# Preparing the expert layer's token operands in units 4 to 7 and keeping them in DRAM, in a decoder layer on one Trainium2 core

## The chip, the cores and the metric

The kernel runs on one core of one Trainium2 (trn2) chip. The metric is the device time of one execution in microseconds (us). Six instruction streams matter here: PE (TensorE, the matmul engine, with its weight loads shown apart as PEld), DVE (VectorE), ACT (ScalarE), POOL (GpSimd), and SP, the queue from which nearly all DMA transfers are issued. Each engine works through its own instructions in order and waits at semaphores for the others.

## What is computed

A decoder layer over 2 x 2048 tokens of width 512, in float32: linear attention, cross attention on a short context, and a mixture of experts. Only the last part is touched by the change:

```python
def _L0_ffn_ref(hidden_states, router_w, w_gate, w_up, w_down, ws_gate, ws_up, ws_down):
    TOP_K = 6
    def _glu_mlp(x, wg, wu, wd):
        return jax.nn.silu(x @ wg) * (x @ wu) @ wd
    B, S, D, E, F, FS = (2, 1024, 512, 8, 256, 512)
    ...
    x = hidden_states.reshape(-1, D)
    scores = jax.nn.softmax(x @ router_w, axis=-1)
    topk_w, topk_idx = jax.lax.top_k(scores, TOP_K)
    g = jnp.einsum('td,edf->etf', x, w_gate)
    u = jnp.einsum('td,edf->etf', x, w_up)
    f_all = jnp.einsum('etf,efd->ted', jax.nn.silu(g) * u, w_down)
    ...
    y = jnp.sum(picked * topk_w[:, :, None], axis=1).reshape(B, S, D)
    y = y + _glu_mlp(hidden_states, ws_gate, ws_up, ws_down)
    return y
x = x + _L0_attn_ref(_layernorm(x, axis=-1), ...)
x = x + _L0_xattn_ref(_layernorm(x, axis=-1), ctx_1024, ctx_1024, ...)
x = x + _L0_ffn_ref(_layernorm(x, axis=-1), ...)
```

All eight experts are computed for every token; the router's softmax, cut to the six best experts, gives the weights (gates) of the sum. A shared expert is added.

## The kernel before

**Tiles and stages.** The 4096 tokens are eight blocks of `TB` = 512 tokens, each four tiles of 128 tokens. Attention and cross attention run first, block by block, and leave the residual stream of block b in DRAM as `x2[b]`. Then comes the expert stage, which starts at about 1042 us of the span. It takes the blocks in four groups of two (g = 0, 2, 4, 6). For each group it goes through ten units u: eight experts and the shared expert in two halves. That makes forty (group, unit) pairs n = 0 to 39, the list `todo3`; group 2 begins at n = 10, group 4 at n = 20, group 6 at n = 30.

**Exact matmuls in three terms.** An operand is held as a pair: a rounded high half (`nc.scalar.copy` into a float32r tile on ACT) and a low half, the original less the high half (`low`, line 118, on DVE or POOL). A product takes three matmuls (`TERMS`): high x high, low x high, high x low.

**Seven parts per unit.** The gate and up products of a unit for two blocks are made by a scheme of the Strassen-Winograd kind with `NP` = 7 products in place of 8. Part s (`products`, matmul at line 1053) multiplies a weight operand `wq` with a token operand `xo` of 128 x 1024 values in a pair (`xops[g, s]`). Two parts use the transposed tokens of the first block directly, one those of the second, four use sums and differences. Each part is 12 matmuls of 128x512, so a unit has 84. The down products add 42 per unit in the same form (`down_products`, line 1166, sums gathered on DVE at line 1187), interleaved with the next unit's parts. In group 0 (n = 0 to 9, "early") weights come raw and their operands are made on ACT, DVE and POOL and stored to DRAM for the later groups (`prepare`, `down_sums`), and down products take 48 matmuls per unit in plain form (`down`, line 148). Later groups load the finished weight operands (`load_until`, at most three uses ahead of program order).

**Preparing the next group, before the change.** In unit 8 of a group `expert_ahead(b)` loads the eight tiles of the next two blocks of `x2`, normalizes them (`normalize`, lines 245 to 252: statistics and scaling on DVE, a power on POOL; pinned in program order), turns them with PE transposes (line 802) and copies them with ACT into `raws[b]`, 8 KB per partition and block (line 803). Sixteen matmul ticks after a block's last tile `route(b)` makes its router scores (line 815), copies them out with DVE (`ls`, line 824), and 22 ticks later `rank(b, ls)` turns them back (line 833), takes the softmax and compares each expert with each other one to keep the best six (lines 842 to 861, DVE with two steps on POOL). `store_gates` writes the gates to DRAM (lines 871 to 875), from where later groups load them as rows (`gr`, line 1103). In unit 9 `tokens_part(g, s)`, called once after each part, makes the seven token operands for the next group out of `raws`: subtractions on POOL (line 1015), the high half on ACT (line 1035), the low half on DVE (line 118, tile `xo`).

**Order.** `dense` is a list of generators that emit PE's matmuls one by one; `dense.after(n, f)` calls f after n further matmuls. This sets the program order. The framework then orders each engine's instructions by a simulated timeline, with program order as priority; an instruction made under `keep_in_program_order` (also called `held`) stays in its place. DMA loads on SP can stand far ahead of their use, as far as free buffers allow.

**Buffers.** `big` has 17 buffers of 8 KB per partition (`eight`): token operands, weight operands, raw weights, `raws`. `work` has 4 pairs (`pair_of`, tag `hl`), 9 single tiles (`half`, tag `kp`) and 5 row tiles (tag `xs`, for loaded token tiles and gate rows). PSUM has 4 banks for parts (`ps`) and 4 for everything else (`sc`).

Of the kernel before, what the change touches and what calls it, by code (L numbers as in the profile page):

```python
# [17 lines left out]
P = 128  # L18
# [19 lines left out]
def decoder_layer(  # L38
# [62 lines left out]
    def half(name, dtype=F32):  # L101
        return work.tile([P, 512], dtype, tag="kp", name=name, bufs=9)
# [664 lines left out]
    for s in range(ws_gate.shape[1] // F):  # L767
# [14 lines left out]
        base=0,  # L782
        channel_multiplier=0,
    )
    accs, raws, gates = {}, {}, {}
# [24 lines left out]

    def route(b):

        pl = sc.tile([P, TB], F32, tag="sc", name=f"pl{b}")
        for k in range(NC):
            nc.tensor.matmul(
                pl[k * HD : (k + 1) * HD, :],
                lhsT=rw[:, k, :],
                rhs=raws[b][:, k, :],
                start=True,
                stop=True,  # L820
                skip_group_check=True,
            )
        ls = half(f"ls{b}")
        nc.vector.tensor_copy(ls, pl)
        dense.after(22, lambda: rank(b, ls))

    def rank(b, ls):


        gates[b] = small.tile([P, NT, E], F32, tag="gates", bufs=4, name=f"gates{b}")  # L830
        pr = sc.tile([P, NT, NC, HD], F32, tag="sc", name=f"pr{b}")
        for t in range(NT):
            nc.tensor.transpose(
                pr[:, t].rearrange("p k e -> p (k e)"), ls[:, t * P : (t + 1) * P], ident
            )
        wide = [P, NT, E]

        def little(tag, shape):
            return small.tile(shape, F32, tag=tag, name=f"{tag}{b}", bufs=1)

        lg = little("lg", wide)
        nc.vector.tensor_reduce(lg, pr[:, :, :, :E].rearrange("p t k e -> p t e k"), AX.X, ALU.add)
        m = little("m", [P, NT])
        nc.vector.tensor_reduce(m, lg, AX.X, ALU.max)
        s = little("s", wide)
        nc.vector.tensor_tensor(s, lg, m.unsqueeze(2).to_broadcast(wide), ALU.subtract)
        nc.scalar.activation(s, s, AF.Exp)
        nc.vector.tensor_reduce(m, s, AX.X, ALU.add)
        nc.vector.reciprocal(m, m)
        nc.vector.tensor_tensor(s, s, m.unsqueeze(2).to_broadcast(wide), ALU.mult)  # L850
        rk = little("rank", wide)
        mine = s.unsqueeze(3).to_broadcast([P, NT, E, E])
        other = s.unsqueeze(2).to_broadcast([P, NT, E, E])
# [4 lines left out]
        nc.gpsimd.tensor_tensor(eq, eq, before.unsqueeze(1).to_broadcast([P, NT, E, E]), ALU.mult)  # L858
        nc.gpsimd.tensor_tensor(gt, gt, eq, ALU.add)
        nc.vector.tensor_reduce(rk, gt, AX.X, ALU.add)  # L860
        nc.vector.scalar_tensor_tensor(gates[b], rk, float(TOPK), s, ALU.is_lt, ALU.mult)
        if b >= GROUP:
            dense.after(60, lambda: store_gates(b))

    gated = {g: dram.tile([E, GROUP, TB], F32, name=f"gated{g}") for g in range(GROUP, nblk, GROUP)}

# [17 lines left out]
    todo3 = [  # L884
        (range(g, g + 2), u) for g in range(0, nblk, 2) for u in range(len(units))
    ]
    NP = 7
    KH = NC // 2
    quarter = [P, 2, KH, P]
    DH = D // 2  # L890
    LAST = len(todo3) - 1
# [116 lines left out]

    def tokens_part(g, s):

        lo, hi = slice(0, KH), slice(KH, NC)

        def less(dst, a, b):
            if g:
                held(nc.gpsimd.tensor_tensor(dst, a, b, ALU.subtract))
            else:
                nc.vector.tensor_tensor(dst, a, b, ALU.subtract)

        r0, r1 = raws[g], raws.get(g + 1)
        xop = xops[g, s] = eight([P, 2, KH, TB], FR, f"xo{g}_{s}")  # L1020
# [436 lines left out]
    for n, (group, u) in enumerate(todo3):  # L1457
        early_group = n < len(units)
        g = group[0]
        more = group[-1] + 1 < nblk  # L1460
        ahead = [[], []]
        if u == len(units) - 2 and more:
            ahead = [expert_ahead(b) for b in range(group[-1] + 1, group[-1] + 3)]
        parts = products(n) if n else ready
        downs = [[] for _ in range(NP)]
        if n > len(units):
            downs = [[d] for d in down_products(n - 1)]
        if u == 1 and n > len(units) + 1:
# [119 lines left out]
```

## Time and profile before

| what | value |
|---|---|
| median of three runs | 2346.76 us (2346.34 to 2348.77) |
| the profiled execution | 2340.21 us |
| its span in the trace | 2338.5 us |
| mean granted PE clock | 0.984 |
| DMA traffic | 485.63 MB, mean 208 GB/s |
| chain that ended last: PE at line 1053 (`pg`) | 25% of the span |
| the same, PE at line 1166 (`pf`) | 10% of the span |
| first part of unit n = 0, 10, 20, 30 starts at | 1042.3, 1417.5, 1715.8, 2021.8 us |

The page counts an engine as busy while one of its instructions runs; matmuls are pipelined, so a busy PE can still run slowly. A wait is put down to the instruction whose semaphore came last. The expert stage takes 1296 of the 2338.5 us. A window is a stretch of the span; its row gives each engine's busy time in it.

### The profile page before, as it was taken

How to read it: one execution, taken by the hardware profiler on the slowest of the kernel's cores; microseconds unless marked ns; L12 is line 12 of the kernel's file. 1: busy time of each engine (PE TensorE's matmuls, PEld its weight loads, DVE VectorE, ACT ScalarE, POOL GpSimd, SP SyncE). 2: the span in 40 equal slices, each digit the busy share in tenths (PEclk: the TensorE clock that was granted, in tenths of full speed). 3: DMA queues.
4: the chain of work that ended last, by engine and by line, in shares of the span. 5: the costliest groups of instructions: out<-in, count | busy, mean ns of one | idle time of the engine just before them, and what ended most of it. 6: DMA issues, size and time to landing. Idle time of an engine off the chain costs nothing.

```text
span 2338.5 us, 35133 instructions
## 1 busy us (share of the span) xinstructions
PE 2241.0 (96%) x11978; PEld 1733.3 (74%) x11978; DVE 1680.3 (72%) x2777; ACT 1104.9 (47%) x2598; POOL 1223.2 (52%) x1086
## 2 busy tenths in 40 slices
PE   7999999899989999999999999999999999999999
PEld 5888777655577777766777777888778887788887
DVE  6554555668577776877877786777887778977777
ACT  4555776756566766775343333222333222432221
POOL 5545433547475554553655554544564455754543
PEclk9999999999999999999999999999999999999999
DMA  6555778899965665565665646555447556575553
GB/s 210 180 171 174 208 210 228 248 255 266 258 201 159 173 175 155 172 199 203 243 240 221 223 175 258 209 222 207 158 180 275 207 207 236 193 276 202 211 189 131
DMA packets 194896, 485.63 MB, mean 208 GB/s; under 512 B 26970, under 2 KB 46810, under 8 KB 174782
## 3 DMA queue, kind: packets, MB, share of 16 engines
q1 hardware_dynamic: 192990, 477.30, 61.5%
q0 software_dynamic: 1728, 6.09, 0.9%
q8 instruction: 95, 1.56, 0.3%
q14 instruction: 83, 0.68, 0.1%
HBM read 345.01 MB, written 138.31 MB: 207 GB/s over the span
## 4 chain that ended last, share of the span: by engine, by line
PE 48%; DVE 9%; DMA 5%; POOL 4%; issue 3%; ACT 2%; SPq 0%; ACTq 0%; DVEq 0%; POOLq 0%
PE pg L1053 25%; PE pf L1166 10%; PE po_x L148 3%; PE pf L148 2%; PE xpq L148 2%; PE pc L745 2%; PE xpt L725 1%; PE psc L693 1%; DMA rgu<-in_w_up 1%; DVE u L1073 1%; DVE xo L118 1%; POOL hp L118 1%; DVE wq L118 1%; DVE u L1085 1%; DMA xsx<-x 1%
## 5 line engine op out<-in xcount | busy, mean ns | idle before, releaser
L1053 PE MATMUL pg<-xo,wq 128*128 128x512 f32 x3360 | 825.7, 393 | 7.2 <-ACT s L1064 3.5
L1053 PEld LDWEIGHTS pg<-xo,wq 128*128 128x128 f32 x3360 | 630.2, 189 | 149.3 <-ACT s L1064 7.1
L1187 DVE TENSOR_TENSOR sum<-sum,pf 128x512 f32<-128x512 f32 x376 | 250.5, 682 | 61.1 <-PE pf L1166 53.5
L407 POOL TENSOR_TENSOR kacc<-kacc,e_k 128x512 f32<-128x512 f32 x128 | 165.9, 1297 | 225.6 <-DVE e_k L366 203.6
L703 ACT ACTIVATE xe<-psc,nb 128x154 f32<-128x154 f32 x512 | 194.4, 403 | 63.0 <-DVE nb L700 47.4
L708 POOL TENSOR_TENSOR xe<-xe,sm 128x616 f32<-128x616 f32 x128 | 156.7, 1232 | 108.1 <-DVE sm L707 73.7
L1116 POOL TENSOR_TENSOR u<-u,gr 128x512 f32<-128x512 f32 x48 | 63.8, 1328 | 255.7 <-DVE u L1085 244.3
L1166 PE MATMUL pf<-ht,wdo 128*128 128x512 f32 x696 | 187.4, 393 | 1.0 <-DVE sum L1187 1.0
L366 DVE SCALAR_TENSOR_TENSOR e_k<-pp,e_k 128x512 f32<-128x512 f32 x128 | 87.4, 685 | 107.9 <-ACT e_k L365 101.8
L1166 PE MATMUL pf<-hb,wdo 128*128 128x512 f32 x522 | 148.2, 399 | 6.0 <-DVE sum L1187 5.9
L1166 PEld LDWEIGHTS pf<-ht,wdo 128*128 128x128 f32 x696 | 129.8, 188 | 30.7 <-DVE sum L1187 1.7
L1084 ACT ACTIVATE u<-u 128x512 f32<-128x512 f32 x80 | 50.6, 633 | 211.1 <-DVE u L1073 208.5
L148 PE MATMUL pf<-wd,hp 128*128 128x512 f32 x528 | 134.0, 400 | 6.2 <-DVE hp L118 3.0
L700 DVE TENSOR_REDUCE nb<-psc 128x2 f32<-128x308 f32 x256 | 111.9, 467 | 31.1 <-PE psc L693 30.9
L148 PEld LDWEIGHTS pf<-wd,hp 128*128 128x128 f32 x528 | 99.7, 190 | 33.1 <-DVE hp L118 3.9
L1166 PEld LDWEIGHTS pf<-hb,wdo 128*128 128x128 f32 x522 | 97.4, 189 | 30.4 <-DVE sum L1187 7.7
L1073 DVE TENSOR_TENSOR u<-u,pg 128x512 f32<-128x512 f32 x160 | 107.7, 679 | 10.5 <-PE pg L1053 9.7
L703 ACT ACTIVATION_READ_ACCUMULATOR xe<-psc,nb 128x1 f32 x512 | 111.6, 218 | 0.0
L364 ACT ACTIVATE e_k<-pp 128x512 f32<-128x512 f32 x128 | 76.8, 601 | 69.9 <-PE pp L402 64.4
L693 PEld LDWEIGHTS psc<-xkst,xst 96*128 96x128 f32 x512 | 76.1, 193 | 35.2 <-ACT xe L703 18.9
L693 PE MATMUL psc<-xkst,xst 96*128 96x154 f32 x512 | 90.3, 284 | 12.3 <-ACT xe L703 8.4
L402 PEld LDWEIGHTS pp<-pst,kst 96*128 96x128 f32 x512 | 75.8, 191 | 26.8 <-issue 9.9
(280 smaller groups left out, 5143.2 us busy)
## 6 DMA issues: line engine op xcount, KB each, us to landing
wq<-wqs SPq DMA_DIRECT2D x90, 1024.0 KB
wqs<-wq SPq DMA_DIRECT2D x30, 1024.0 KB
wdo<-wds SPq DMA_DIRECT2D x29, 1024.0 KB
kst<-kd SPq DMA_DIRECT2D x96, 256.0 KB
qst<-qd SPq DMA_DIRECT2D x96, 256.0 KB
xst<-xqd SPq DMA_DIRECT2D x96, 256.0 KB
wdo<-wds SPq DMA_DIRECT2D x29, 768.0 KB
kd<-khl SPq DMA_DIRECT2D x32, 512.0 KB
```

Of the source, the lines that this page charges most:

```text
L148: nc.tensor.matmul(dst, lhsT=a, rhs=b, start=n == 0, stop=n == len(todo) - 1)
L364: nc.scalar.activation(e, src, AF.Relu, scale=-1.0)
L366: nc.vector.scalar_tensor_tensor(e, src, 0.0, e, ALU.max, ALU.add)
L407: nc.gpsimd.tensor_tensor(acc, acc, kp, ALU.add)
L693: nc.tensor.matmul(psc[:, i], lhsT=xsts[b, c][:, h, t * P : (t + 1) * P], rhs=ksts[bt, c][:, h, :], start=True, stop=True,)
L700: nc.vector.tensor_reduce(nb[:, two], psc, AX.X, ALU.max, negate=True)
L703: nc.scalar.activation(e[:, h, :], psc[:, i], AF.Exp, bias=nb[:, h : h + 1], accum_out=sm[:, h : h + 1],)
L708: nc.gpsimd.tensor_tensor(e, e, sm.unsqueeze(2).to_broadcast([P, 4, keys]), ALU.mult)
L1053: nc.tensor.matmul(pb, lhsT=w[:, p, i, k, :], rhs=xop[:, q, k, :], start=first and m == 0, stop=m == len(todo) - 1, skip_group_check=True,)
L1073: nc.vector.tensor_tensor(dst, dst, pb, ALU.add)
L1166: nc.tensor.matmul(banks[i], lhsT=w[:, p, i * P : (i + 1) * P], rhs=t[q], start=new and m == 0, stop=m == len(TERMS) - 1, skip_group_check ...
L1187: nc.vector.tensor_tensor(dst, dst, banks[i], ALU.add)
```

## The change

The preparation of groups 2, 4 and 6 is taken apart into small pieces and spread over earlier units:

- **Layernorms** of blocks 2 to 7 (`normalize_ahead`): one tile at a time, 24 in all, at parts 2 and 5 of units n = 0 to 3 and at part 5 of units n = 4 to 19. The normalized tile is stored in DRAM (`xn2`). They are no longer pinned.
- **Token operands** of the next group (`operands_ahead`): 24 pieces, one after each part from part 1 of unit 4 to part 3 of unit 7. They come in two halves q of 12 pieces: four that load and turn tiles of `xn2` (a quarter of the next two blocks' values each, as 16 loads of 128 KB per group), one for router scores, seven for the operands. A half operand is 128 x 512, made by ACT and DVE in a `pair_of` tile and stored in DRAM (`xod`); eight subtractions of 128 x 512 per group run on POOL.
- **Unit 9**: `tokens_part` for later groups only loads the finished operand, one DMA of 1 MB.
- **Routing**: the scores of two blocks stand in one tile of double width; softmax and ranking run once per group instead of once per block, with single steps further apart. This holds for group 0 too, where one `routed(0)` takes the place of two. Scores are copied out by ACT instead of DVE.

The diff, without the parts that only move:

```diff
+    xod = {}
+    xn2 = {b: dram.tile([TB, D], F32, name=f"xn2_{b}") for b in range(GROUP, nblk)}
...
-            xs = load_tile(x2[b], 0, t, f"f{b}_")
-            made[t] = normalize(xs, f"f{b}_{t}", pinned=b > 1)
+            made[t] = normalize(load_tile(x2[b], 0, t, f"f{b}_"), f"f{b}_{t}")
...
-            if t == NT - 1 and b > 1:
-                dense.after(16, lambda: route(b))
...
+    def normalize_ahead(b, t):
+        xs = normalize(load_tile(x2[b], 0, t, f"n{b}_"), f"n{b}_{t}")
+        dense.after(8, lambda: nc.sync.dma_start(out=tile_of(xn2[b], 0, t), in_=xs))
+        yield from ()
+
+    def operands_ahead(g):
+        turned, tiles, firsts = {}, {}, []
+
+        def load(q, j, t2):
+            xs = work.tile([P, 2, 2, P], F32, tag="xs", name=f"xq{g}_{q}_{j}_{t2}", bufs=5)
+            for i in range(2):
+                nc.sync.dma_start(
+                    out=xs[:, i],
+                    in_=tile_of(xn2[g + j], 0, 2 * t2 + i).rearrange(
+                        "p (h q n) -> p h q n", h=2, q=KH
+                    )[:, :, q],
+                )
+            tiles[q, j, t2] = xs
+
+        def turn(q, j, t2):
+            if (j, t2) == (0, 0):
+                turned[q] = eight([P, GROUP, 2, TB], F32, f"xt{g}_{q}")
+            xs = tiles.pop((q, j, t2))
+            pt = sc.tile([P, 2, 2, P], F32, tag="sc", name=f"ptf{g}_{q}_{j}_{t2}")
+            for h in range(2):
+                for i in range(2):
+                    nc.tensor.transpose(pt[:, h, i, :], xs[:, i, h, :], ident)
+            nc.scalar.copy(
+                turned[q][:, j, :, 2 * t2 * P : 2 * (t2 + 1) * P],
+                pt.rearrange("p h i n -> p h (i n)"),
+            )
...
+        def scores(q):
+            pl = sc.tile([P, TB], F32, tag="sc", name=f"pl{g}_{q}")
...
+            ls = half(f"ls{g}_{q}")
+            nc.scalar.copy(ls, pl)
+            dense.after(14, lambda: add_scores(q, ls))
+            yield from ()
...
+        def operand(q, n):
+            (b11, b21), (b12, b22) = ([turned[q][:, j, h] for h in range(2)] for j in range(GROUP))
+
+            def less(dst, a, b):
+                nc.gpsimd.tensor_tensor(dst, a, b, ALU.subtract)
+
+            if n == 2:
+                less(b11, b12, b11)
+                src = half(f"t2_{g}_{q}")
+                less(src, b22, b11)
+                less(b21, b21, src)
+            elif n == 3:
+                less(b12, b22, b12)
+                src = b12
+            else:
+                src = (b11, b21, None, None, b21, b11, b22)[n]
+            hl = pair_of(f"xo{g}_{n}_{q}")
+            nc.scalar.copy(hl[:, 0], src)
+            low(hl[:, 1], src, hl[:, 0])
+            dense.after(
+                6, lambda: nc.sync.dma_start(out=xod[g, n][:, :, q, :], in_=hl.bitcast(F32))
+            )
+            yield from ()
+
+        parts = []
+        for q in range(KH):
+            parts += [turns(q, n) for n in range(4)] + [scores(q)]
+            parts += [operand(q, n) for n in range(NP)]
+        return parts
...
-        nc.vector.tensor_copy(ls, pl)
-        dense.after(22, lambda: rank(b, ls))
+            ls.append(half(f"ls{b + j}"))
+            nc.scalar.copy(ls[j], pl)
+        dense.after(14, lambda: turn_scores(b, ls))
...
+        nc.scalar.activation(s, s, AF.Exp)
+        dense.after(14, lambda: rank(b, s, m))
...
-        both = half(f"gteq{b}").rearrange("p (i t e j) -> p i t e j", i=2, t=NT, e=E)
+        both = pair_of(f"gteq{b}").bitcast(F32)
...
+        dense.after(40 if b else 14, chosen)
...
+        xop = xops[g, s] = eight([P, 2, KH, TB], FR, f"xo{g}_{s}")
+        if g:
+            nc.sync.dma_start(out=xop.bitcast(F32), in_=xod[g, s])
+            return
...
-    dense.add(outs[0], routed(0), routed(1), outs[1], prepare(0, 1), tokens_part(0, 2), outs[2])
+    dense.add(outs[0], routed(0), outs[1], prepare(0, 1), tokens_part(0, 2), outs[2])
...
-        ahead = [[], []]
-        if u == len(units) - 2 and more:
-            ahead = [expert_ahead(b) for b in range(group[-1] + 1, group[-1] + 3)]
+        if u == 0 and more:
+            ahead = operands_ahead(group[-1] + 1)
...
-            if ahead[0]:
-                (ln, tr), (ln2, tr2) = ahead
-                todo = (ln, [], tr[:2], tr[2:] + ln2, [], tr2[:2], tr2[2:])
-                dense.add(*todo[s])
+            if s == 5 or s == 2 and n < 4:
+                at = 2 * n + s // 3 if n < 4 else n + 4
+                if at < (nblk - GROUP) * NT:
+                    dense.add(normalize_ahead(GROUP + at // NT, at % NT))
+            if more and u * NP + s > GROUP * NT // 2 * NP and ahead:
+                dense.add(ahead.pop(0))
```

More of the change, by code (lines that the diff above doesn't have):

```diff
@@ L784, in decoder_layer @@
     )
+    NP = 7
+    KH = NC // 2
     accs, raws, gates = {}, {}, {}
+    xod = {}
+    xn2 = {b: dram.tile([TB, D], F32, name=f"xn2_{b}") for b in range(GROUP, nblk)}
     def expert_ahead(b):
@@ L805, in turn @@
             yield
-            if t == NT - 1 and b > 1:
-                dense.after(16, lambda: route(b))
         return [values(t) for t in range(NT)], [turn(t) for t in range(NT)]
-    def route(b):
[L813 to L821, printed above, removed]
-            )
-        ls = half(f"ls{b}")
-        nc.vector.tensor_copy(ls, pl)
-        dense.after(22, lambda: rank(b, ls))
@@ L827, in rank @@
[L827 to L843, printed above, removed]
+    def normalize_ahead(b, t):
+        xs = normalize(load_tile(x2[b], 0, t, f"n{b}_"), f"n{b}_{t}")
+        dense.after(8, lambda: nc.sync.dma_start(out=tile_of(xn2[b], 0, t), in_=xs))
+        yield from ()
@@ new lines, in operands_ahead, with turns, add_scores @@
+    def operands_ahead(g):
[22 more added lines that the diff above has]
+            )
+        def turns(q, n):
+            if n == 0:
+                load(q, 0, 0)
+            if n < 3:
+                load(q, *divmod(n + 1, 2))
+            turn(q, *divmod(n, 2))
+            yield
+            yield
+        def scores(q):
+            pl = sc.tile([P, TB], F32, tag="sc", name=f"pl{g}_{q}")
+            for j in range(GROUP):
+                for h in range(2):
+                    at = (2 * j + h) * HD
+                    nc.tensor.matmul(
+                        pl[at : at + HD, :],
+                        lhsT=rw[:, h * KH + q, :],
+                        rhs=turned[q][:, j, h, :],
+                        start=True,
+                        stop=True,
+                        skip_group_check=True,
+                    )
[3 more added lines that the diff above has]
+            yield from ()
+        def add_scores(q, ls):
+            lg = little("lg" if q else "lg0", g)
+            pr = sc.tile([P, NT, GROUP, 2, HD], F32, tag="sc", name=f"pr{g}_{q}")
+            for t in range(NT):
+                nc.tensor.transpose(
+                    pr[:, t].rearrange("p j h e -> p (j h e)"), ls[:, t * P : (t + 1) * P], ident
+                )
+            for j in range(GROUP):
+                nc.vector.tensor_reduce(
+                    lg[:, j * NT : (j + 1) * NT],
+                    pr[:, :, j, :, :E].rearrange("p t h e -> p t e h"),
+                    AX.X,
+                    ALU.add,
+                )
+            if q == 0:
+                firsts.append(lg)
+            else:
+                nc.vector.tensor_tensor(lg, lg, firsts.pop(), ALU.add)
+                dense.after(8, lambda: softmax(g, lg))
+        def operand(q, n):
[10 more added lines that the diff above has]
+                src = b12
+            else:
+                src = (b11, b21, None, None, b21, b11, b22)[n]
[4 more added lines that the diff above has]
+                6, lambda: nc.sync.dma_start(out=xod[g, n][:, :, q, :], in_=hl.bitcast(F32))
+            )
+            yield from ()
[4 more added lines that the diff above has]
+        return parts
@@ new lines, in route @@
+    def route(b):
+        ls = []
+        for j in range(GROUP):
+            pl = sc.tile([P, TB], F32, tag="sc", name=f"pl{b + j}")
+            for k in range(NC):
+                nc.tensor.matmul(
+                    pl[k * HD : (k + 1) * HD, :],
+                    lhsT=rw[:, k, :],
+                    rhs=raws[b + j][:, k, :],
+                    start=True,
+                    stop=True,
+                    skip_group_check=True,
+                )
+            ls.append(half(f"ls{b + j}"))
+            nc.scalar.copy(ls[j], pl)
+        dense.after(14, lambda: turn_scores(b, ls))
@@ new lines, in turn_scores @@
+    def turn_scores(b, ls):
+        lg = little("lg", b)
+        for j in range(GROUP):
+            pr = sc.tile([P, NT, NC, HD], F32, tag="sc", name=f"pr{b + j}")
+            for t in range(NT):
+                nc.tensor.transpose(
+                    pr[:, t].rearrange("p k e -> p (k e)"), ls[j][:, t * P : (t + 1) * P], ident
+                )
+            nc.vector.tensor_reduce(
+                lg[:, j * NT : (j + 1) * NT],
+                pr[:, :, :, :E].rearrange("p t k e -> p t e k"),
+                AX.X,
+                ALU.add,
+            )
+        softmax(b, lg)
@@ L844, in rank, with softmax, little @@
+    def softmax(b, lg):
+        m = small.tile([P, GROUP * NT], F32, tag="m", name=f"m{b}", bufs=1)
         nc.vector.tensor_reduce(m, lg, AX.X, ALU.max)
-        s = little("s", wide)
+        s = little("s", b)
         nc.vector.tensor_tensor(s, lg, m.unsqueeze(2).to_broadcast(wide), ALU.subtract)
         nc.scalar.activation(s, s, AF.Exp)
+        dense.after(14, lambda: rank(b, s, m))
+    wide = [P, GROUP * NT, E]
+    def little(tag, b):
+        return small.tile(wide, F32, tag=tag, name=f"{tag}{b}", bufs=1)
@@ L848, in rank @@
+    def rank(b, s, m):
+        two = small.tile(wide, F32, tag="gates", bufs=2, name=f"gates{b}")
         nc.vector.tensor_reduce(m, s, AX.X, ALU.add)
@@ L850, in rank @@
         nc.vector.tensor_tensor(s, s, m.unsqueeze(2).to_broadcast(wide), ALU.mult)
-        rk = little("rank", wide)
-        mine = s.unsqueeze(3).to_broadcast([P, NT, E, E])
-        other = s.unsqueeze(2).to_broadcast([P, NT, E, E])
-        both = half(f"gteq{b}").rearrange("p (i t e j) -> p i t e j", i=2, t=NT, e=E)
+        rk = little("rank", b)
+        every = [P, GROUP * NT, E, E]
+        mine = s.unsqueeze(3).to_broadcast(every)
+        other = s.unsqueeze(2).to_broadcast(every)
+        both = pair_of(f"gteq{b}").bitcast(F32)
+        both = both.rearrange("p i (t e j) -> p i t e j", e=E, j=E)
         gt, eq = both[:, 0], both[:, 1]
@@ L857, in rank, with chosen @@
         nc.vector.tensor_tensor(eq, other, mine, ALU.is_equal)
-        nc.gpsimd.tensor_tensor(eq, eq, before.unsqueeze(1).to_broadcast([P, NT, E, E]), ALU.mult)
+        nc.gpsimd.tensor_tensor(eq, eq, before.unsqueeze(1).to_broadcast(every), ALU.mult)
         nc.gpsimd.tensor_tensor(gt, gt, eq, ALU.add)
[L860 to L863, printed above, removed]
+        def chosen():
+            nc.vector.tensor_reduce(rk, gt, AX.X, ALU.add)
+            nc.vector.scalar_tensor_tensor(two, rk, float(TOPK), s, ALU.is_lt, ALU.mult)
+            for j in range(GROUP):
+                gates[b + j] = two[:, j * NT : (j + 1) * NT]
+                if b >= GROUP:
+                    dense.after(60 + 12 * j, lambda at=b + j: store_gates(at))
+        dense.after(40 if b else 14, chosen)
     gated = {g: dram.tile([E, GROUP, TB], F32, name=f"gated{g}") for g in range(GROUP, nblk, GROUP)}
@@ L886, in decoder_layer @@
     ]
-    NP = 7
-    KH = NC // 2
+    xod.update(
+        ((g, n), dram.tile([P, 2, KH, TB], F32, name=f"xod{g}_{n}"))
+        for g in range(GROUP, nblk, GROUP)
+        for n in range(NP)
+    )
     quarter = [P, 2, KH, P]
@@ L1009, in tokens_part @@
     def tokens_part(g, s):
+        xop = xops[g, s] = eight([P, 2, KH, TB], FR, f"xo{g}_{s}")
+        if g:
+            nc.sync.dma_start(out=xop.bitcast(F32), in_=xod[g, s])
+            return
         lo, hi = slice(0, KH), slice(KH, NC)
         def less(dst, a, b):
[L1014 to L1017, printed above, removed]
+            nc.vector.tensor_tensor(dst, a, b, ALU.subtract)
         r0, r1 = raws[g], raws.get(g + 1)
-        xop = xops[g, s] = eight([P, 2, KH, TB], FR, f"xo{g}_{s}")
         if s == 0:
```

## The prediction

> **What bounds the kernel now.** I read the page's engine shares first, then a table of windows cut at unit boundaries, then the instructions of TensorE (PE) and VectorE (DVE) around the widest holes.
>
> ```profile
> PE 2241.0 (96%) x11978; PEld 1733.3 (74%) x11978; DVE 1680.3 (72%) x2777; ACT 1104.9 (47%) x2598; POOL 1223.2 (52%) x1086
> ```
>
> PE sets the pace, so a change pays only where PE waits. The windows (length, then busy time and instructions of PE, weight load, DVE, ScalarE, GpSimd; granted clock; DMA share; GB/s) are expert units: n = 1, 2, 3, 4, 8, 9, 19, 27, 28, 29.
>
> ```profile
> 1110.80:1144.10 33.30, 30.87 (x133) 24.61 (x132) 27.81 (x34) 12.71 (x22) 22.50 (x19) 1.00 0.67 245
> 1144.10:1176.90 32.80, 31.32 (x134) 24.59 (x133) 25.93 (x32) 13.68 (x24) 22.00 (x17) 1.00 0.62 229
> 1176.90:1208.30 31.40, 30.68 (x134) 24.68 (x133) 24.08 (x32) 11.80 (x20) 17.98 (x15) 1.00 0.66 247
> 1208.30:1238.90 30.60, 30.60 (x134) 24.70 (x133) 22.38 (x31) 11.75 (x20) 16.44 (x14) 1.00 0.62 228
> 1332.00:1362.30 30.30, 29.79 (x138) 24.05 (x137) 25.34 (x45) 10.26 (x19) 14.02 (x21) 1.00 0.69 235
> 1362.30:1417.50 55.20, 46.09 (x205) 35.03 (x204) 48.79 (x71) 26.13 (x41) 34.10 (x28) 0.91 0.44 169
> 1672.40:1715.80 43.40, 38.98 (x182) 29.52 (x181) 37.20 (x63) 19.60 (x28) 25.48 (x19) 0.92 0.34 118
> 1923.90:1952.80 28.90, 28.90 (x127) 23.66 (x126) 20.65 (x33) 7.68 (x14) 14.83 (x11) 1.00 0.53 209
> 1952.80:1980.00 27.20, 27.20 (x126) 22.24 (x125) 25.90 (x47) 8.36 (x15) 14.97 (x19) 1.00 0.61 218
> 1980.00:2021.80 41.80, 39.53 (x194) 29.61 (x193) 39.20 (x67) 19.25 (x30) 26.74 (x21) 1.00 0.47 164
> ```
>
> Unit 27 is the undisturbed yardstick: 84 + 42 = 126 wide matmuls in 28.90 us, 0.229 us each. Unit 9 holds 205 records, 48 of them routing (16 score matmuls, 32 transposes). In the order of PE's instructions four transposes take 0.36 us net and the eight score records of a block 1.0 us, so routing costs 2 x 1.0 + 8 x 0.36 = 4.9 us, and 157 x 0.229 + 4.9 = 40.9 us would do: **14.3 us lost**. Unit 19: 182 - 48 = 134, 30.7 + 4.9 = 35.6, 7.8 us lost. Unit 29 (52 small records): 142, 32.5 + 5.3 = 37.8, 4.0 us lost. The same sum gives 0.9 us for unit 8, about 0 for 18 and 28, and 4.8 us for 20, 21, 30 and 31 together. **About 32 us** lie around the three group changes. PE's own rows there:
>
> ```profile
> 1372.65 1.12 PE L833 MATMUL pr<-ident,ls 128*128 128x128 f32 x4 [5.48 <-DVE ls L824]
> ...
> 1414.27 3.45 PE L148 MATMUL pf<-wd,hp 128*128 128x512 f32 x8 [2.72 <-DVE hp L118]
> ...
> 1689.43 1.65 PE L1166 MATMUL pf<-hb,wdo 128*128 128x512 f32 x3 [4.21 <-DVE sum L1187]
> ...
> 1998.54 0.96 PE L1166 MATMUL pf<-hb,wdo 128*128 128x512 f32 x3 [1.40 <-DVE sum L1187]
> ```
>
> All four wait for DVE. In DVE's order, layernorms precede the late score copy of 1371.91, two operand subtractions (xo, L118) directly precede the late hp of 1413.54, and ranking steps and an xo subtraction of 2.30 us precede the late sum of 1688.70. This is the work the diff moves.
>
> **The change, part by part.** Removed from units 8 and 9 of groups 0 to 2, per change: eight layernorms and eight transposed copies; two score copies, two rankings, seven 128x1024 operands (rounded copy on ScalarE, low half on DVE) and four subtractions on GpSimd. In return, seven 1 MB loads.
>
> ```profile
> L245 DVE BATCH_NORM_STATS2 st_f<-xsf x24: 679/685/692, 1344.3 to 1985.7; 128x6 f32<-128x512 f32 x24
> ...
> L252 DVE TENSOR_SCALAR xsf<-xsf,mv_f,rs_f x24: 527/544/1516, 1346.8 to 1992.7; 128x512 f32<-128x512 f32 x24
> ...
> L118 DVE TENSOR_TENSOR xo<-xt,xo x24: 1207/1290/2300, 1047.3 to 2034.9; 128x1024 fp32r<-128x1024 f32 x24
> ...
> L118 DVE TENSOR_TENSOR hb<-s,hb x29: 673/684/1781, 1445.7 to 2287.8; 128x512 fp32r<-128x512 f32 x29
> ```
>
> The rows (shortest, median and longest ns) give DVE's part: 8 x 1.40 (0.685, an aggregation of 0.173, 0.544) = 11.2 us, 7 x 1.29 = 9.0, two copies of 0.677 and two rankings of about 2.9 (ten steps of 0.17 to 0.43): 27.4 us per change, nearly twice what PE loses there even at 14.3. The gain lies between 11.1 us (only the waits of 5.48, 4.21 and 1.40) and 32. I take **25**: unit 9 keeps about 3 us because it ends the early form of the unit, where down products need fresh activations, and units 19 to 31 some 4.
>
> The rows of units 9 and 19 show a granted clock of 0.91 and 0.92 around their 5.48 and 4.21 us holes, 1.00 where holes stay under 3. The Trainium skill, "TensorE: Matmul & The Clock Gate", Part 1, says that an idle window of about 3.4 us halves the clock until PE has been busy as long; by it each of the two long holes costs some 1.7 us more in slow matmuls (an estimate from that page), so the least gain would be 14.5 in place of the rows' 11.1; the 25 counts such losses already, being taken from lengths.
>
> **Layernorms** (24, in units 0 to 19). Two in each of units 0 to 3, so 2.8 us of DVE and 2 x 0.79 (0.222 + 0.567) of GpSimd per unit. These units are not free: 132 wide matmuls need 30.3, so units 1, 2 and 3 lose 3.0, 2.5 and 1.1 us while DVE works 27.8, 25.9, 24.1. From unit 3 to unit 1 that is 1.9 us for 3.7 us of DVE, 0.5 per us: 2.8 x 0.5 x 4 = 5.6, less 1 for group 0's two rankings made one. Bounds 0 (loads run ahead into idle DVE time) and 11.2 (all of it exposed). I take **+4**, near the slope. Each adds a 256 KB store on SP.
>
> **Operands, units 4 to 7.** Per group DVE gets 14 x 0.684 = 9.6 us, and scores and ranking at double width: four 128x64 reduces of about 0.22 (between the 0.173 and 0.288 of neighbours), an addition and the softmax steps at 0.17 to 0.19 (1.2), two comparisons at 0.68, a reduce at 0.68, a product at 0.2: 13.9 us over 24 slots (3.4 units), 4.0 a unit, and 1.4 for a layernorm. GpSimd gets 8 x 1.3 + 2 x 1.3 = 13 us, 3.8 a unit; ScalarE 8 x 0.59 + 14 x 0.62 + 2 x 0.6 = 14.6 us, on an engine 40% busy. PE's transposes and score matmuls are the same number, moved. In units 4 to 7 DVE rises from 22.4 to 28 us of 30.6 and GpSimd from 16.4 to 21, the load of units 1 and 2. With their slope: 5.4 x 0.5 x 4 = 10.8. With unit 8's row (25.34 of DVE for 0.9 lost, against 0.3 in unit 4, slope 0.2): 4.3. Bounds 0 and 18; I take **+6**. In groups 1 and 2 cover is better: units 18 and 28 ran 26.34 and 25.90 us of DVE without a hole, and DVE goes from about 21 to 25 or 27; bounds 0 and 12, I take **+2**.
>
> The top of these bounds is the GpSimd row: a low half of 128x512 takes 0.684 us alone and 1.24 on average where GpSimd runs the early units' sums (wq<-rgu, units 4 to 7); 14 x 0.56 = 7.8 on top of 10.8. The Trainium skill, "SBUF — State Buffer", Who interferes with whom, gives the reason and speaks against this change: a DVE instruction with two SBUF inputs and a GpSimd instruction that reads SBUF lock each other out for a whole instruction. If every one of the 42 new lows met such a lock at the row's 0.56, the sum would be 42 x 0.56 = 23.5 us worse, +11 in place of -13 (an estimate); the median of 684 says that most lows of the later units meet none.
>
> **Transfers and queues.** Per group 16 loads of 128 KB, 14 stores of 512 KB, 7 loads of 1 MB, 8 stores of 256 KB. Units 4 to 7 get 9.3 MB; at 8192 B in 0.32 us on 16 engines (410 GB/s) that is 23 us in 104, a DMA share of 0.62 becoming 0.85. Unit 19 gets 7.3 MB, 18 us, on 0.34 x 43.4 = 14.8: 33 us in some 36. It fits, barely; each operand has a unit until use. Cost **0**, and 7.7 if the first load of each group is exposed (three of 2.6 us). SP issues in order: 45 more issues of 0.3 to 0.5 us a group. A store waiting for a late low holds up the raw-weight loads behind it; in units 5 and 6 SP's own waits show six for such a low (wq), 40.8 us, the longest 7.4. Cover: prepared weights precede their use by some 14 us (loaded at 1250, used from 1270); gone, each unit pays the wait, up to 7.4.
>
> Sum: -25 + 4 + 6 + 2 + 0 = **-13 us**. The profiled execution is 2340.2 us (span 2338.5), 6.6 below the median of the runs, 2346.8; I take off 13 from the median: **2334 us**.
>
> **Rivals.**
> 1. *The added work hides entirely.* For: units 18 and 28. Against: units 1 to 3. Gain 28 to 32: 2317 us. Chance 0.20.
> 2. *The holes belong to the change of groups, not to routing.* Then only the 11.1 us of named waits return, the costs of 12 stand: 2348 us, no change. Against: the DVE order above. 0.12.
> 3. *DVE becomes the bound in the early units (slower).* Place: units 0 to 7; it decides once DVE with GpSimd's locks passes the 30.3 us of PE, which at 28 needs 2.3 more, four stretched lows a unit. Price 11 + 18 + 6 later, against a gain of 18: +17, 2364 us. 0.20.
> 4. *Four operand pairs are too few (slower).* hb, hp and ht hold three to four of the four "hl" buffers; now seven operands a unit each hold one until a 512 KB store lands. A rounded copy waiting for one holds ScalarE, behind which PE's banks are emptied. 12 units at 1 to 2 us, 18, on top of -13: +5, 2352 us. 0.10.
>
> My forecast, 2325 to 2342, has 0.38. A measurement here tells 0.2%, 4.7 us, from no change. Faster: 0.38 + 0.20 = 0.58; same 0.12; slower 0.30. The range, 2316 to 2362, leaves out the tails of rivals 1 and 3.
>
> **What would show it.** Right: units 9, 19 and 29 below 44, 37 and 39 us with clock 1.00, no PE hole over 2 us there, units 4 to 7 at 31 to 33. Wrong: units 4 to 7 above 34, waits of PE for DVE there or for xt loads, or unit 19 over 40 with PE waiting for xo from DMA.

## The result

| kernel | median us | runs |
|---|---|---|
| before | 2346.22 (2342.53 to 2351.09) | 20 |
| after | 2352.02 (2342.62 to 2363.41) | 20 |

The ratio is 1.0028, interval 1.0018 to 1.0038: the change makes the kernel 0.28% slower, some 6 us. The forecast was 2334 us, faster.

Both spans hold an attention stage of a length that changes from execution to execution: unit 0 starts at 1042.3 and 1055.9 us in two profiles of the kernel before, at 1053.6 and 1048.6 in two of the kernel after. The expert stage, from there to the end, can be compared: 1296.2 and 1296.2 us before, 1298.8 and 1301.6 after. So the expert stage grew, by 2.6 to 5.4 us. Whether the attention stage also differs in the mean can't be told from two profiles each.

The page's line of engine shares, of the kernel after:

```profile
PE 2245.8 (95%) x11978; PEld 1732.5 (74%) x11978; DVE 1682.5 (72%) x2763; ACT 1109.4 (47%) x2619; POOL 1225.9 (52%) x1090
```

TensorE has as many records as before, and DVE as much work. The windows of the kernel after (columns as in the prediction) are units n = 1, 4, 7, 9, 16, 17, 19, 27 and 29:

```profile
1120.50:1158.50 38.00, 33.12 (x133) 25.54 (x132) 34.50 (x50) 14.86 (x26) 31.06 (x31) 0.96 0.85 299
...
1220.80:1253.60 32.80, 32.80 (x148) 24.75 (x147) 24.48 (x35) 15.06 (x27) 17.18 (x16) 1.00 0.75 265
...
1323.00:1359.70 36.70, 33.66 (x141) 26.41 (x140) 30.84 (x45) 16.98 (x28) 23.75 (x19) 0.95 0.74 273
...
1393.30:1432.80 39.50, 39.14 (x170) 31.47 (x169) 27.58 (x40) 9.91 (x17) 12.49 (x13) 1.00 0.99 390
...
1602.00:1635.00 33.00, 32.80 (x139) 23.21 (x138) 25.33 (x37) 11.71 (x21) 18.04 (x14) 1.00 0.72 263
1635.00:1668.70 33.70, 30.18 (x132) 23.40 (x131) 32.39 (x51) 12.35 (x21) 23.50 (x22) 1.00 0.67 256
...
1699.60:1728.40 28.80, 28.80 (x127) 23.67 (x127) 21.24 (x34) 7.35 (x14) 9.43 (x7) 1.00 0.98 392
...
1943.20:1978.60 35.40, 32.68 (x143) 26.27 (x143) 32.12 (x49) 14.78 (x24) 21.84 (x17) 0.95 0.61 216
...
2007.40:2037.70 30.30, 30.30 (x134) 24.83 (x133) 22.57 (x35) 8.87 (x15) 10.04 (x7) 1.00 0.94 359
```

Units 9, 19 and 29 run without a hole worth the name (0.36 us in all in unit 9), at 39.5, 28.8 and 30.3 us and full clock: the expected gain is there. It is spent in the units that took the work. Unit 17 has 3.5 us of holes of TensorE and 32.39 us of DVE in 33.70; unit 27 is alike. Units 4 and 16 hold no such holes, and are longer all the same.

A unit's **loss** below is its length less 0.2294 us per wide matmul, 0.09 per transpose and 0.125 per score record (each score matmul leaves two records). Unit 0 also ends the cross attention, whose matmuls have no such price, so for units 0 to 3 only the difference is given. Summed in us:

| units | before | after | difference |
|---|---|---|---|
| 0 to 3 | - | - | +1.3 |
| 4 to 8 | 3.9 | 14.8 | +10.9 |
| 9, 10 | 14.9 | 0.8 | -14.1 |
| 14 to 18 | 0.1 | 11.7 | +11.6 |
| 19 to 21 | 10.8 | 2.0 | -8.8 |
| 24 to 28 | 0.3 | 9.0 | +8.7 |
| 29 to 31 | 7.3 | 0.4 | -6.9 |

Gains of 29.8 us stand against costs of 32.5: but for rounding, the 2.6 us between the two first profiles. In the second profile of the kernel after, units 14 to 18 lose 13.9 in place of 11.7. TensorE's own waits from unit 0 on, in the kernel after (in all, times, longest, us), are too small for the costs (the five largest groups; in units 4 to 8, 14 to 18 and 24 to 28 all its waits make up 13.1 of the 35.5 us lost):

```profile
PE pf L148 <- DVE mv_n L248: 3.4, 1, 3.4
PE pf L148 <- DVE acc L1386: 3.3, 4, 2.8
PE pgt L1008 <- DVE gates L994: 2.7, 1, 2.7
PE pg L1193 <- DMA wq<-wqs: 2.7, 4, 1.5
PE pg L1193 <- ACT s L1204: 2.4, 3, 1.4
```

Part of the loss is in no wait at all. TensorE's timeline (start, length, then line, operation and count of adjacent records) shows one such place: first the kernel before in unit 19, then the kernel after in unit 16.

```profile
1673.72 1.07 PE L1053 MATMUL pg<-xo,wq 128*128 128x512 f32 x4
1674.72 1.06 PE L815 MATMUL pl<-xt,rw 128*32 128x512 f32 x8
1675.72 0.66 PE L802 MATMUL ptf<-ident,xsf 128*128 128x128 f32 x4
```

```profile
1618.27 1.04 PE L862 MATMUL pl<-xt,rw 128*32 128x512 f32 x2
1619.24 1.65 PE L1193 MATMUL pg<-xo,wq 128*128 128x512 f32 x6
1620.73 0.86 PE L1306 MATMUL pf<-hb,wdo 128*128 128x512 f32 x3
1621.52 1.05 PE L862 MATMUL pl<-xt,rw 128*32 128x512 f32 x2
1622.50 1.19 PE L1193 MATMUL pg<-xo,wq 128*128 128x512 f32 x4
1623.62 1.05 PE L862 MATMUL pl<-xt,rw 128*32 128x512 f32 x2
...
1625.49 1.04 PE L862 MATMUL pl<-xt,rw 128*32 128x512 f32 x2
```

Four score matmuls, each 32 columns wide in a column group of its own, advance TensorE by 1.00 us when they are adjacent (1674.72 to 1675.72). One alone, with wide matmuls on both sides, advances it by 0.97 (1618.27 to 1619.24). Call a stretch of adjacent score matmuls a run. Before, the scores stood in 8 runs of four; after, the framework's order has cut them into 16 runs. That makes eight more microseconds a theory to test. (Transposes, which moved too, advance TensorE by 0.09 to 0.10 us each as before.)

### The profile page after: what moved, and what is told of

Its sections match the earlier page's. It is cut to its first block, busy times and chain, and to the rows that moved or that the text cites. A ratio compares the mean times of both kernels' runs of the same rounds, so it can differ in the third digit from the quotient of the medians.

```text
span 2352.4 us, 35396 instructions
## 1 busy us (share of the span) xinstructions
PE 2245.8 (95%) x11978; PEld 1732.5 (74%) x11978; DVE 1682.5 (72%) x2763; ACT 1109.4 (47%) x2619; POOL 1225.9 (52%) x1090
## 4 chain that ended last, share of the span: by engine, by line
PE 70%; DMA 13%; DVE 9%; issue 3%; POOL 2%; ACT 1%; SPq 1%; DVEq 0%; POOLq 0%; ACTq 0%
PE pg L1193 27%; PE pf L1306 10%; PE pf L148 4%; PE pq L148 3%; PE pk L148 3%; PE pv L148 3%; PE xpq L148 3%; PE po_x L148 3%; PE pc L745 2%; PE pp L402 2%; PE xpt L725 2%; PE psc L693 2%; DMA zr<-zd 2%; DMA qst<-qd 2%; PE pkv L230 1%
## 5 line engine op out<-in xcount | busy, mean ns | idle before, releaser
L148 PEld LDWEIGHTS pf<-wd,hp 128*128 128x128 f32 x528 | 99.7, 190 | 35.5 <-DVE acc L1386 5.4
```

The source lines that it names most:

```text
L148: nc.tensor.matmul(dst, lhsT=a, rhs=b, start=n == 0, stop=n == len(todo) - 1)
```

## The experiments

Stage is the expert stage of the profiled execution; ratios are to the kernel before, measured beside each. The two profiles of the kernel after differ by 2.8 us of stage, so a smaller difference between two stages, or between two sums of losses, tells nothing by itself.

### e1_scores: the score matmuls together again

```diff
         def scores(q):
+            dense.after(8, lambda: score(q))
+            yield from ()
+        def score(q):
...
-                    nc.tensor.matmul(
+                    columns.matmul(
```

`columns.matmul` holds the order. The scores are issued eight matmuls later, so that all four operands are there.

> The changed kernel with the router-score matmuls of groups 2, 4 and 6 emitted 8 ticks later and kept in program order, so that a half's four stay next to each other on PE (8 runs of score matmuls in place of 16; nothing left out). Theory A, scattered scores: a run of score matmuls takes about 1.0 us whether it holds two records or eight, since the four write to different column groups and overlap only when adjacent; 8 runs fewer give about 8 us, so some 2344 us, ratio to before 0.998 to 1.000, and units 4, 6, 14, 16, 24, 26 lose 1 to 3 us less each. Rival B, DVE load: the score matmuls cost nothing that matters, the time stays at 2350 to 2354, ratio 1.002 to 1.004.

Measured: 8 runs of score matmuls, stage 1291.5 us, 2342.55 us, ratio 0.9983 (0.9969 to 0.9997). The stage is 7.3 us below that of the kernel after (10.1 below its second profile), for eight runs fewer, and the kernel is now faster than the one before, by 0.17%. Units 14 to 18 lose 7.7 us, 24 to 28 6.1; 4 to 8, where a hole of 3.86 us came in at 1338.02, still 15.1.

### e9_scatter: the same score matmuls apart

```diff
+            for k in range(1, 2 * GROUP):
+                dense.after(2 * k, lambda k=k: one(*divmod(k, 2)))
+            one(0, 0)
+            dense.after(4 * GROUP, lambda: copied(q, pl))
```

> As e1_scores, but in the three later groups each of a block's four score matmuls is issued two expert matmuls after the one before it, and the copy of the scores follows the last: 25 runs of score matmuls in TensorE's order in place of 8, with the same number of them and the same work on every other engine. Theory A (a run takes about 1.0 us of TensorE whether it holds one matmul or four): 17 runs more at 1.0 us, the expert stage at 1306 to 1310 us against the 1291.5 of e1_scores, time some 17 us above it, ratio to before near 1.0055. Rival (where the scores stand does not matter, and e1_scores gained by making the copies and softmaxes later): stage within 3 us of 1291.5, ratio 0.997 to 1.000.

Measured: 25 runs, stage 1308.8 us, 2357.71 us, ratio 1.0063 (1.0038 to 1.0087). TensorE's timeline of this kernel:

```profile
1626.18 1.04 PE L230 MATMUL pl<-xt,rw 128*32 128x512 f32 x2
1627.15 0.73 PE L1203 MATMUL pg<-xo,wq 128*128 128x512 f32 x2
1627.82 1.04 PE L230 MATMUL pl<-xt,rw 128*32 128x512 f32 x2
```

17 runs more than in e1_scores cost 17.3 us. The loss grows by 3.9, 5.9 and 5.9 us in the three stretches, which hold 5, 6 and 6 more runs. So the eight extra runs of the kernel after cost it some eight microseconds; in its own trace, TensorE advances by 13.7 us over the score matmuls of those three stretches, where e1_scores needs 6.0.

### e2_noln and e8_noln2: no layernorm arithmetic for blocks 2 and 3

Both leave out the arithmetic of the layernorms of blocks 2 and 3 (tiles loaded and stored unchanged); e2_noln from the kernel after, e8_noln2 from e1_scores.

```diff
-        xs = normalize(load_tile(x2[b], 0, t, f"n{b}_"), f"n{b}_{t}")
+        xs = load_tile(x2[b], 0, t, f"n{b}_")
+        if b >= 2 * GROUP:
+            normalize(xs, f"n{b}_{t}")
```

> The changed kernel without the layernorm arithmetic of blocks 2 and 3 (their tiles are loaded and stored as they are in units 0 to 3). Theory C, layernorms in the tight early units: unit 1 loses about 4.6 us more than before the change, with PE waiting 3.4 us behind a layernorm step; without the eight layernorms units 0 to 3 come back to at most their earlier loss, and the time falls by 3 to 5 us, to 2347 to 2349. Rival: unit 1 loses the same to its other DVE work, the time falls by under 1.5 us.

> The kernel of e1_scores without the layernorm arithmetic of blocks 2 and 3 (left out; their tiles are loaded and stored). With the scores in order in both. Theory C: PE's wait of 3.4 us in unit 1 goes, units 0 to 3 lose 2 to 5 us less, stage 1286.5 to 1289.5. Rival: DVE's other work fills the place, under 1.5 us.

Measured: e2_noln 2344.81 us, ratio 0.9992 (0.9975 to 1.0009), stage 1296.4; e8_noln2 2340.33, ratio 0.9984 (0.9969 to 1.0000), stage 1290.3. The first can't be read: its order also changed the runs of score matmuls from 16 to 13. The second has 8 like e1_scores. Units 0 to 3 lose 3.4 us less than in e1_scores, but units 14 to 18 give 2.0 back, and the stage is 1.2 us shorter, as the rival had it. The layernorms cost about 3 us where they stand; at the end no cost can be told from the spread of a stage.

### e3_nolow and e6_nolow2: no low halves

The low half of the later groups' operands is a second copy on ScalarE, not a subtraction on DVE; e3_nolow from the kernel after, e6_nolow2 from e1_scores.

```diff
-            low(hl[:, 1], src, hl[:, 0])
+            nc.scalar.copy(hl[:, 1], src)
```

> The changed kernel with the low halves of the later groups' token operands made by a second ACT copy in place of the DVE subtraction (the subtraction is left out; 42 DVE instructions fewer, 42 ACT copies more, the same transfers). Theory B, DVE load in units 4 to 7: those units (and 14 to 17, 24 to 27) lose about 9, 7 and 7 us more than before the change beside the scattered scores; without the lows half to all of that returns, 10 to 20 us, ratio to before 0.995 to 0.999. Theory A (scores): the lows are hidden, under 4 us return, ratio 1.001 or more.

> The kernel of e1_scores with the low halves of the later groups' token operands made by a second ACT copy in place of the DVE subtraction (the subtraction is left out). With the scores in order in both, this is the price of the 42 lows on DVE alone. Theory B: units 4 to 8, 14 to 18 and 24 to 28 of e1_scores lose about 11, 7 and 6 us more than before the change; the lows are over half of DVE's new work there, so 8 to 14 us return, stage 1277 to 1284. Rival: they are hidden, the stage stays over 1288.

Measured: e3_nolow 2339.19 us, ratio 0.9963 (0.9949 to 0.9977), stage 1285.2, with 14 runs of score matmuls, so two of the 13.6 us that its stage is shorter are theirs. e6_nolow2, with 8 runs, 2331.70 us, ratio 0.9947 (0.9926 to 0.9967), stage 1282.6: 8.9 us below e1_scores. The low halves on DVE cost some 9 us. Without them units 24 to 28 lose 1.6 us (6.1 in e1_scores), units 14 to 18 5.9 (7.7). These rows of the kernel after say why they are dear (DVE's groups in units 4 to 8, 14 to 18 and 24 to 28; busy us, mean ns):

```profile
L118 DVE TENSOR_TENSOR xo<-xt,xo 128x512 fp32r<-128x512 f32 x12 | 10.9, 920 | 0.1
```

```profile
L118 DVE TENSOR_TENSOR xo<-xt,xo 128x512 fp32r<-128x512 f32 x12 | 14.2, 1193 | 0.2 <-ACT xo L912 0.2
```

```profile
L118 DVE TENSOR_TENSOR xo<-xt,xo 128x512 fp32r<-128x512 f32 x12 | 15.0, 1254 | 4.1 <-ACT xo L912 4.0
```

With two more per group from `t`, 14 lows took 13.6, 16.2 and 17.3 us, where the prediction had 14 x 0.684 = 9.6. In the trace, 10 of the 42 overlap with no instruction of GpSimd and took 0.67 to 0.68 us; 24 took 1.04 to 1.86, every one beside a GpSimd instruction (the other 8 met one too, and took at most 0.81). One of them, on DVE and then GpSimd:

```profile
1604.58 1.79 DVE L118 TENSOR_TENSOR xo<-xt,xo 128x512 fp32r<-128x512 f32 x1
```

```profile
1604.04 1.77 POOL L1256 TENSOR_TENSOR u<-u,gr 128x512 f32<-128x512 f32 x1 [0.77 <-ACT hb L1249]
```

Only 4 of the 24 stand beside the change's own subtractions (L899). The others met work that GpSimd had before as well: the multiplications by the gates (`gr`), sums, and low halves of other tiles.

### e7_big: pairs from another pool

```diff
-            hl = pair_of(f"xo{g}_{n}_{q}")
+            hl = eight([P, 2, TB], FR, f"xop{g}_{n}_{q}")
```

From e1_scores; tests whether four pairs are too few.

> The kernel of e1_scores with each half operand made in a buffer of the large pool in place of one of the four pairs (nothing left out). Rival 4 of the prediction, too few pairs: ACT and DVE waited some 10 us in all for stores of operands (the longest 1.8 us); with other buffers those waits go and the stage falls by 3 to 8 us, to 1283 to 1288. If the waits lie in idle time of ACT: 1290 to 1293, or more if weight loads come late for want of large buffers.

Measured: 2339.51 us, ratio 0.9987 (0.9973 to 1.0000), stage 1292.9 against 1291.5, with 9 runs of score matmuls. Units 4 to 8 gain 2.2 us, unit 9 and the later ones lose 3.8: no gain over e1_scores.

### e5_rank: the comparisons in halves

```diff
+        for k in range(4):
+            dense.after(1 + 6 * k, lambda k=k: compare(*divmod(k, 2)))
...
-        dense.after(40 if b else 14, chosen)
+        dense.after(46 if b else 24, chosen)
```

> The kernel of e1_scores with the two comparisons of the joint ranking, 128x512 each on DVE, made as four of 128x256, each six ticks after the one before (nothing left out). Theory D, the joint ranking: in e1_scores PE still waits 3.4 us in unit 17 and 3.9 us in unit 7 while DVE works through two comparisons of 1.2 to 1.75 us in a row ahead of the emptying of a PSUM bank; with short ones apart, units 7 and 17 lose 3 us less each and the expert stage falls from 1291.5 to about 1285 to 1288 us. Rival B, DVE load alone: another instruction takes their place in front, the stage stays at 1290 to 1293.

Measured: 2338.17 us, ratio 0.9982 (0.9967 to 0.9998), stage 1294.3, with 9 runs of score matmuls: no gain, holes of 4.06 and 3.53 us stay. But the test missed its aim. DVE's timeline of group 4's ranking has the four halves as one entry:

```profile
1634.09 3.57 DVE L993 TENSOR_TENSOR gteq<-s 128x256 f32<-128x256 f32 x4
```

The framework put them back to back (so in group 2, and two by two in group 6), and next to nothing was spread.

### e10_late and e11_gates: the ranking behind the low halves

DVE's timeline of e1_scores in unit 17, ahead of TensorE's hole of 3.36 us at 1641.69:

```profile
1634.41 0.65 DVE L1330 TENSOR_TENSOR sum<-sum,pf 128x512 f32<-128x512 f32 x1
1634.98 0.19 DVE L981 RECIPROCAL m<-m 128x8 f32<-128x8 f32 x1
1635.09 1.41 DVE L118 TENSOR_TENSOR ht<-sg,ht 128x512 fp32r<-128x512 f32 x1
1636.43 0.21 DVE L982 TENSOR_TENSOR s<-s,m 128x64 f32<-128x64 f32 x1
1636.56 0.68 DVE L1330 TENSOR_TENSOR sum<-sum,pf 128x512 f32<-128x512 f32 x1
1637.16 1.75 DVE L990 TENSOR_TENSOR gteq<-s 128x512 f32<-128x512 f32 x1
1638.84 1.74 DVE L991 TENSOR_TENSOR gteq<-s 128x512 f32<-128x512 f32 x1
1640.51 0.53 DVE L252 TENSOR_SCALAR xsn<-xsn,mv_n,rs_n 128x512 f32<-128x512 f32 x1
1640.97 0.67 DVE L1210 TENSOR_TENSOR u<-s,pg 128x512 f32<-128x512 f32 x1
```

No entry has an idle time. The addition `u<-s,pg` of 1640.97, which frees TensorE's bank, stands behind a low half, a layernorm step and two comparisons of 1.75 us, each beside a GpSimd instruction (0.68 to 0.69 where none runs). (The other hole, at 1338.02, turned out to wait for ScalarE, which had waited 2.48 us for GpSimd.) Both kernels are e1_scores with the ranking moved:

```diff
-        dense.after(14, lambda: rank(b, s, m))
+        dense.after(104 if b else 14, lambda: rank(b, s, m))
```

e10_late also shortens the two distances behind it, from 40 and 60 to 24 and 24; e11_gates leaves them.

> As e1_scores, but the ranking of the three later groups is started 104 expert matmuls after its softmax in place of 14, so that it stands behind the last low half of the group in VectorE's order, in unit 8, 18 and 28; the steps behind it follow faster. In e1_scores VectorE is busy without a gap from 1623 to 1641 us, and TensorE waits 3.86 us (1338.02) and 3.36 us (1641.69) behind the two comparisons. Theory D (the lows and the ranking in one stretch are what overfills VectorE): both holes fall below 1.5 us, the expert stage at 1284 to 1287 us against 1291.5, time 2335 to 2338, ratio near 0.9960. Rival L (the lows fill VectorE by themselves, and the ranking only happens to stand at the end of the queue; halving its comparisons in e5_rank left holes of 4.06 and 3.53): a hole over 2.5 us stays in units 7 and 17, before another instruction, stage 1289 to 1293.

> As e10_late, but with the steps behind the ranking at the distances of e1_scores (40 expert matmuls to the choice, 60 to the gates' transposes, in place of 24 and 24). In e10_late TensorE, in order, waited 6.70 and 11.22 us for the gates before their transposes (pgt, 1675.69 and 1993.48), while units 7 and 17 lost 4.6 and 1.2 us less than in e1_scores. If those two waits came from the shortened distances alone: no wait of TensorE over 1 us before pgt, units 18 and 28 back below 33 us, the expert stage at 1286 to 1291 us, time 2337 to 2342, ratio 0.9965 to 0.9985. If GpSimd's two steps of the ranking are late wherever the ranking stands behind the lows: a wait over 3 us stays before pgt, stage above 1295, ratio above 1.000.

Measured: e10_late 2362.98 us, ratio 1.0079 (1.0061 to 1.0096), stage 1311.7; e11_gates 2341.02, ratio 0.9958 (0.9941 to 0.9974), stage 1288.9. TensorE's waits in e10_late, and in e11_gates from 1300 to 2000 us:

```profile
PE pgt L1011 <- DVE gates L997: 17.9, 2, 11.2
```

```profile
PE pg L1196 <- DVE u L1216: 3.7, 3, 2.2
PE pg L1196 <- DMA wq<-wqs: 2.1, 3, 1.3
PE pf L148 <- DVE hp L118: 1.4, 1, 1.4
```

e10_late shows what a distance is worth: TensorE takes its instructions in order and stood 17.9 us at the gates' transposes, a loss of its edit alone, since e11_gates has no such wait. With the distances kept, units 14 to 18 lose 5.4 us (7.7 in e1_scores) and 24 to 28 4.1 (6.1). Group 0 gains nothing: units 4 to 10 lose 18.0 us in place of 15.2. In all the stage is 2.6 us shorter than that of e1_scores, within the spread of repeats: that the place of the ranking costs something is likely, not shown. e1_scores and e11_gates beat the kernel before; e11_gates has the lower ratio, though the two were measured against different runs of it, and their intervals overlap.

### after_again and before_again: second profiles

> The changed kernel once more, unchanged, for its profile. Up to unit 0 every engine's order is that of the kernel before, yet unit 0 began 11.3 us later in the profiled execution. If that is a chance of the execution, unit 0 begins anywhere from 1042 to 1056 us here and in the other runs of this batch; if it belongs to the program (the place of its buffers in DRAM, say), it begins at 1052 to 1055 again. The expert stage itself, from unit 0 to the end, was 1296.2 us before and 1298.8 after, and should be 1297 to 1301 again.

> The kernel before, unchanged, for a second profile. If the length of the attention stage is a chance of the execution, unit 0 starts anywhere from 1041 to 1054 us and the expert stage is 1295 to 1298 us again. If the changed kernel is what makes the attention stage longer (1053.6 and 1048.6 in its two profiles against 1042.3), unit 0 starts at 1041 to 1044.

Measured: after_again 2351.93 us, unit 0 at 1048.6, stage 1301.6; before_again 2353.77 us, unit 0 at 1055.9, stage 1296.2. The attention stage is as long as chance has it with either kernel (in the ten kernels of the other experiments unit 0 starts between 1041.2 and 1054.3), and the expert stage before repeats to 0.1 us. The expert stage after repeats to 2.8.

## Why the prediction failed

The sum was -25 + 4 + 6 + 2 + 0 = -13. What the two first profiles of the stage gave, term by term:

| term | predicted | measured | from |
|---|---|---|---|
| group changes, units 9, 10, 19 to 21, 29 to 31 | -25 | -29.8 | losses |
| layernorms, units 0 to 3 | +4 | +1.3 | losses |
| operands, units 4 to 8 | +6 | +8.9 | 10.9 less 2 extra runs of scores |
| operands, units 14 to 18 and 24 to 28 | +2 | +14.3 | 20.3 less 6 extra runs |
| score matmuls | 0 | +8 | 8 runs at 1.0 us |

**Right: where TensorE lost time and why.** The holes at the group changes belonged to DVE's preparation of the next group, and moving it returned nearly all of the 32 us. The signs named for it came: units 9, 19 and 29 below 44, 37 and 39 us, clock 1.00, no hole over 2 us. So did a sign of being wrong, units 4 to 7 above 34 us with waits for DVE: units 6 and 7 took 35.5 and 36.7. The rival that gave the holes to the change of groups itself is out. The rival that the added work hides entirely is out as well, by costs of 32.5 us.

Transfers at 0 held nearly: unit 9 now moves 390 GB/s without a wait, but waits for `wq` are 2.7 us in all, and 4.7 in the second profile, against 0.7 before. One comes from the order of SP's queue, which the prediction named for late low halves: in unit 17 two stores of normalized tiles waited there for late DVE steps, with the weight loads behind them.

```profile
1647.84 1.74 SPq L815 DMA_DIRECT2D xn<-xsn  x2
1649.67 0.38 SPq L1076 DMA_DIRECT2D wq<-wqs  x1
```

```profile
1654.60 4.38 PE L1193 MATMUL pg<-xo,wq 128*128 128x512 f32 x18 [1.54 <-DMA wq<-wqs]
```

**Wrong: "in groups 1 and 2 cover is better", at +2.** This is the larger of the two failed steps, and 14.3 us lies above even its upper bound of 12. Three parts of its reasoning failed. It spread the load over four units: DVE was to go "from about 21 to 25 or 27", and the mean of units 14 to 17 is indeed 27.8 us, but unit 17 alone has 32.39, since low halves, layernorm steps and the ranking of two blocks come together there. It priced a low half at 0.684 us, because "most lows of the later units meet none" of GpSimd's locks; 24 of 42 were stretched beside a GpSimd instruction, 20 of them by work that it had before as well, and the mean in these units was 1.2 us. The median came from one row (`hb<-s,hb`); another row of the kernel before, also of low halves of 128x512, has a mean of 0.958:

```profile
L118 DVE TENSOR_TENSOR ht<-sg,ht 128x512 fp32r<-128x512 f32 x29 | 27.8, 958 | 15.5 <-ACT ht L1109 15.3
```

And the prediction took units 18 and 28, with 26 us of DVE and no hole, as proof of cover: a unit's sum doesn't say whether work comes in one piece ahead of the instruction that frees a bank. e6_nolow2 puts 9 us on the low halves over all groups, 6.3 of it in these units; e11_gates suggests a further 4.3 us for the place of the ranking, more than a repeat of the stage spreads but from one profile. The rest of the 14.3 stays open.

On the lock the Trainium skill, "SBUF — State Buffer", Who interferes with whom, was the better guide to what a low half takes. By it a DVE instruction with two SBUF inputs contends with a GpSimd instruction that reads SBUF. The prediction worked out 23.5 us from it, as an estimate, and set it aside for the row's median. The lows of the kernel after fit that rule: none was stretched without a GpSimd instruction beside it, and the 42 took 47.1 us, 18 above the 28.7 of a price of 0.684. As a cost of the stage the 23.5 was too high: doing without all 42 returned 8.9 us (e6_nolow2).

**Wrong: "PE's transposes and score matmuls are the same number, moved", at 0.** The number is the same, the cost isn't: a score matmul is nearly free beside its three neighbours and costs 0.97 us alone. The row used, 1.0 us for eight records of a block, held the answer, but a run's price was taken for a price per record. The Trainium skill, "TensorE: Matmul & The Clock Gate", Part 3, has narrow matmuls in separate column tiles running at the same time, which agrees with four in 1.00 us. It gives no price for breaking such a group.

**The sign.** With the scores at 0 the terms give -5.3, the size of e1_scores' gain (-4.7 us of stage). With the operands as predicted, 6 + 2, and the scores at 8 they give -12.5. Only both together make the kernel slower. That -12.5 lies so near the forecast's -13 is luck: 4.8 us more gained at the group changes and 2.7 less lost to layernorms make up for the 8 of the scores.

**Rivals.** "DVE becomes the bound in the early units" had the mechanism, but the wrong place: it was priced at units 0 to 7, and most of it came in units 14 to 27, which were thought safe. "Four operand pairs are too few" is not supported: other buffers gained nothing (e7_big), although single waits for such stores exist.

**Not settled.** What holds units 4 to 10 in group 0 wasn't taken apart: they lose 15.5 us after the change (18.8 before, most of it then in unit 9), 14.1 in e6_nolow2 and 15.2 to 18.0 in e1_scores, e5_rank, e7_big, e8_noln2 and e11_gates; there DVE, ScalarE and GpSimd wait for each other in turn. Nor does the trace say why, in units 4 to 8, 14 to 18 and 24 to 28, some 11 us more than before lie in wide matmuls that merely follow each other more slowly, part of it at a lower clock. The layernorms of units 4 to 19 weren't left out in any run.

## What to carry to other kernels

Price an engine's narrow matmuls by the run and not by the piece, and when such a group is emitted piecemeal, hold it together. When work is moved under another engine's cover, add it up over the few microseconds in front of the instruction that frees a buffer, not over the stage, and at the duration it has beside whatever the other engines do there. A stage whose length varies by chance belongs on one side of the comparison: compare from the first instruction of the changed part.

## What was unexpected of the hardware

- A run of 128x32 by 128x512 score matmuls took 0.97 us for one and 1.00 for four in separate column groups; 17 more runs took 17.3 us.
- The same DVE comparison of 128x512 took 0.68 to 0.69 us in the kernel after in the five cases with no GpSimd instruction beside it, and 1.06, 1.49 and 1.75 in the three with one.
- The attention stage ended between 1041.2 and 1055.9 us over the profiled executions, two of them of one and the same kernel 13.6 us apart, while the expert stage of these two agreed to 0.1. The cause of that spread wasn't followed.
- Holes of 2.82 and 2.72 us took the granted clock of units 7 and 27 of the kernel after to 0.95, while one of 3.36 us left unit 17 of e1_scores at 1.00. So the length of a hole alone doesn't decide it. The Trainium skill, "TensorE: Matmul & The Clock Gate", Part 1, names an idle window of about 3.4 us and calls it free-running; the shorter holes that counted here don't fit the length it names.
